# Row maxima of a softmax brought from columns to rows by two DMAs and a ScalarE copy instead of a TensorE transpose

## The chip, the cores and the metric

The kernel runs on one core of one Trainium2 chip. A time is the device time of one execution in microseconds (us); the time of a kernel is the median over its runs. Beside the runs, one execution was taken with the hardware profiler, and all lines of a profile come from it. The engines are TensorE (PE, its weight loads PEld), VectorE (DVE), ScalarE (ACT), GpSimd (POOL) and SyncE (SP). SP does no arithmetic here: it issues nearly all DMAs.

## The reference

One transformer block over 8 batches of 1024 rows of width 256, in float32, with weights given per batch by a small modulation. Cut to what matters:

```python
h = layernorm(x) * (1 + ca) + sa
lhs, rhs = h * w_lhs, h * w_rhs
scores = einsum('nsd,ntd->nst', lhs, rhs)      # 1024 x 1024 per batch, symmetric
attn = softmax(scores, axis=2)
x = x + ga * einsum('nst,ntd->nsd', attn, h)
h = layernorm(x) * (1 + cb) + sb
x = x + gb * (relu(h @ W1 + b1) @ W2 + b2)     # 256 -> 1024 -> 256
```

The softmax takes the maximum of each row of `scores` off before the exponential.

## The kernel before

**Tiles.** A batch has eight row tiles of 128 rows, called rows 0 to 7 of the batch below. The main loop runs over batches `b` (0 to 7) and, in each, over steps `i` (0 to 7). A step works on several stages at once: it computes the scores of the row two ahead (`direct`), mirrors them into the columns of later rows (the score matrix is symmetric), takes the exponentials of the row one ahead, multiplies exponentials by values for earlier rows, and does part of the feed-forward network of the batch before, in eight column chunks `c`, two in each of the steps 0, 1, 4 and 5.

**Layout of the softmax.** `row_max` (line 463, VectorE) takes the maximum of each of the 128 score rows of a tile: one number on each partition, a column. The exponentials, however, are kept turned, with the softmax's row along the free axis, so the maximum is wanted as a row of 128 numbers, the same on all partitions. `max_turn` (line 468) makes it: TensorE transposes the column, read 128 times over, into a PSUM tile `pm`. `subtract` (line 475, VectorE) takes `pm` off the scores into `pT`, and `exponent` (line 484, ScalarE) takes the exponential.

**Where `max_turn` stands.** In step 5 it is called inside `pair_products(fb, fg, c, turn_max)`, the first layer of the feed-forward network. That function issues the products of chunk `c`, has ScalarE copy the first of them to SBUF (`kept`, line 747), and at its end calls what it was given. The order of step 5 from there on, shortened:

```python
pair_products(fb, fg, c, turn_max)      # c = 2; kept, then max_turn of row 6
pair_relu(c - 1)                        # ScalarE, lines 789 and 790
pair_sums(fb, fg, c); mirror(*ahead); pair_last(fb, fg, c)
subtract(*late)                         # row 6
pair_products(fb, fg, c + 1, None)      # c + 1 = 3; kept again
exponent(*late)                         # row 6
...
pair_last(fb, fg, c + 1)                # TensorE writes pa again: needs kept of c + 1
```

`pair_last` multiplies once more into the first half of `pa`, the PSUM tile that `kept` is copied from. So TensorE may issue it only when that copy is done. Behind it stand the products of row 5 (`po`, line 501).

**Where row 6's maximum is taken.** The end of step 4 reads, shortened: `prepare_blocks(b + 1, 1)`, `weights(late)` (row 5), `row_max(b, 6)`. `prepare_blocks` turns the next batch's normalised rows by `move` (lines 306 and 309): four DMAs write the tile `T_a` to DRAM (`D_a`), and one reads it back as `X_a`. All five go on SP's queue, and the read waits there until the four writes have landed. `mirror` and the turns of the feed-forward tensors (`D_f`, `D_y`) go through the same `move`. Batch 7 has no next batch and leaves this `prepare_blocks` out.

**Order.** Nothing is scheduled freely: `pin` at the end ties each instruction to the one before it on its engine, SP's DMAs included, in the order in which the program issued them.

Of the kernel before, what the change touches and what calls it, by code (L numbers as in the profile page):

```python
# [11 lines left out]
F32 = mybir.dt.float32  # L12
# [5 lines left out]
P = 128  # L18
# [6 lines left out]
def adaln_block_kernel(  # L25
# [13 lines left out]
    nc = tc.nc  # L39
    B, S, D = x.shape  # L40
    INTER = W1.shape[1]
    NT = S // P
# [3 lines left out]
    TH = HALF // P  # L46
# [1 line left out]
    NH = NI // 2  # L48
    V = 32
    NV = P // V  # L50
    DX = D + 4

    const = ctx.enter_context(tc.tile_pool(name="const", bufs=1))
    two = ctx.enter_context(tc.tile_pool(name="two", bufs=2))
    work = ctx.enter_context(tc.tile_pool(name="work", bufs=3))
# [3 lines left out]
    dram = ctx.enter_context(tc.tile_pool(name="dram", bufs=1, space=bass.MemoryType.DRAM))  # L59
# [42 lines left out]
    def load_x0(q, queue):  # L102
# [11 lines left out]
        out=wv[ND : 2 * ND, :], in_=w_rhs.rearrange("a b (k p) -> (a b k) p", p=P)  # L114
# [19 lines left out]
    ident = const.tile([P, P], F32, name="ident")  # L134
# [5 lines left out]
    def warm(n):  # L140
# [9 lines left out]
            name=nc.get_next_instruction_name(),  # L150
# [105 lines left out]
    def prepare_start(b):  # L256
        xg_t[b] = two.tile([P, NT, DX], F32, tag="xg", name=f"xg_{b}")
        nc.gpsimd.memset(xg_t[b][:, :, D : D + 1], 1.0)
# [89 lines left out]
    def prepare_turn(b, g, vector=True):  # L348

        xg, pts = xg_t[b], []  # L350
        lT = lT_t[b, g] = two.tile([P, ND, HALF], F32, tag="lT", name=f"lT_{b}_{g}", bufs=2)
        rT = rT_t[b, g] = two.tile([P, ND, HALF], F32, tag="rT", name=f"rT_{b}_{g}", bufs=2)
        rows = lambda T, k: T[:, k, :].rearrange("p (t a v) -> p t a v", a=NV, v=V)
        for k in range(ND):
            if b > 0:
                pt = pre[b, g][:, k]
            else:
                pt = ps_t.tile([P, HALF], F32, tag="t", name=f"pth_{b}_{g}_{k}")
                for j in range(TH):
                    nc.tensor.transpose(pt[:, ts(j, P)], xg[:, g * TH + j, ts(k, P)], ident)  # L360
                pt = pt.rearrange("p (t a v) -> p t a v", a=NV, v=V)
            pts.append(pt)

        def left(k):
            nc.vector.tensor_scalar(
                rows(lT, k), pts[k], side_col(0, 0, k, b), side_col(0, 1, k, b),
                ALU.mult, ALU.add,
            )


        for k in range(ND):
            if vector:
                left(k)
            q = ND - 1 - k if vector else k
            nc.scalar.activation(
                rows(rT, q), pts[q], AF.Identity,
                scale=side_col(1, 0, q, b), bias=side_col(1, 1, q, b),
            )
        return left
# [13 lines left out]
    def score_row(b, i):  # L393
        if b == 0:
            return first_scores()[:, i].rearrange("p (n v) -> p n v", v=V)
        return sc_t[b].rearrange("p i a j v -> p j (i a) v")[:, i]
# [62 lines left out]
    max_t, pT_t = {}, {}  # L459

    def row_max(b, i):
        m = work.tile([P, 1], F32, tag="m", name=f"m_{b}_{i}")
        nc.vector.tensor_reduce(m, score_row(b, i), AX.XY, ALU.max)  # L463
        max_t[b, i] = m

    def max_turn(b, i):
        pm = ps_t.tile([P, HALF], F32, tag="t", name=f"pm_{b}_{i}")
        nc.tensor.transpose(pm[:, :P], max_t.pop((b, i)).to_broadcast([P, P]), ident)  # L468
        pT_t[b, i] = pm

    def subtract(b, i):

        pm = pT_t.pop((b, i))
        pT = work.tile([P, NT, P], F32, tag="pT", name=f"pT_{b}_{i}")
        nc.vector.tensor_tensor(  # L475
            pT.rearrange("p j (a v) -> p j a v", v=V),
            score_columns(b, i),
            pm[:, :P].rearrange("p (j a v) -> p j a v", j=1, v=V).to_broadcast([P, NT, NV, V]),
            ALU.subtract,
        )  # L480
        pT_t[b, i] = pT

    def exponent(b, i):
        nc.scalar.activation(pT_t[b, i], pT_t[b, i], AF.Exp)  # L484
# [24 lines left out]
    def product_out(b, i):  # L509
        po = po_t.pop((b, i))  # L510
        g, j = divmod(i, TH)
        rl = work.tile([P, 1], F32, tag="rl", name=f"rl_{b}_{i}")
        nc.vector.reciprocal(rl, po[:, D : D + 1])
        x2 = x_tile(b, i)
        nc.vector.scalar_tensor_tensor(x2, po[:, :D], rl, x2, ALU.mult, ALU.add)
        stats(mvb_of(b, g), j, x2, f"b{b}_{i}")
# [3 lines left out]


    XS = D - P + 1
    tsum = const.tile([P, 4, TH, P + 4], F32, name="tsum")
    nc.gpsimd.memset(tsum[:, 1, :, P : P + 1], 1.0)

    def right_sums(b, which):

        xg = xg_t[b]
        b11, b12 = xg[:, 0:TH, P:D], xg[:, 0:TH, 0:P]
        b21, b22 = xg[:, TH:NT, P:D], xg[:, TH:NT, 0:P]  # L530
        t = [tsum[:, n, :, 0:P] for n in range(4)]
        ins = [(b12, b11), (b22, t[0]), (b22, b12), (t[1], b21)]
        for n in which:
            nc.gpsimd.tensor_tensor(t[n], *ins[n], ALU.subtract)
# [4 lines left out]
    def pair_begin(b, i, between=None):  # L539

        W = work.tile([P, 2, D + 4], F32, tag="W", name=f"W_{b}_{i}", bufs=1)
        pp = ps_a.tile([P, HALF], F32, tag="a", name=f"pp_{b}_{i}")
        one, other = halves(pT_t[b, i])
        rows = slice(P, P + XS)
        for out, lhs, h in (
            (pp[:, 0:XS], one, 0), (pp[:, XS : 2 * XS], other, 1)
        ):
            for t in range(TH):
                nc.tensor.matmul(  # L549
                    out, lhsT=lhs[:, t, :], rhs=xg_t[b][:, h * TH + t, P : P + XS],  # L550
                    start=(t == 0), stop=(t == TH - 1),
                )
            if between and h == 0:
                between()
        nc.scalar.copy(W[:, 1, rows], pp[:, 0:XS])
        two_t[b, i] = W, pp
# [22 lines left out]
    def pair_end(b, i):  # L579

        (s2, s4), (s3, a22) = halves(pT_t.pop((b, i))), halves(pT_t.pop((b, i + 1)))
        s1 = two_t.pop("s1")
        pq = ps_a.tile([P, HALF], F32, tag="a", name=f"pq_{b}_{i}")
        pr = ps_a.tile([P, HALF], F32, tag="a", name=f"pr_{b}_{i}")
        for out, lhs, rhs in (
            (pr[:, P : 2 * P], s1, tsum[:, 0, :, 0:P]),
            (pq[:, XS : XS + P], a22, tsum[:, 3, :, 0:P]),
            (pr[:, 2 * P : 3 * P], s3, tsum[:, 2, :, 0:P]),
            (pq[:, 0:XS], s2, tsum[:, 1, :, 0:XS]),
            (pr[:, 0:P], s4, xg_t[b][:, TH:NT, 0:P]),  # L590
        ):
            for t in range(TH):
                nc.tensor.matmul(  # L593
                    out, lhsT=lhs[:, t, :], rhs=rhs[:, t, :],
                    start=(t == 0), stop=(t == TH - 1),
                )
        two_t[b, i] = two_t[b, i][0], pq, pr
# [39 lines left out]
    def spare():  # L637
        if queue:
            queue.popleft()()
# [369 lines left out]
    def first_rows():  # L1009

        pr = ps_a.tile([P, HALF], F32, tag="a", name="prow")
        nc.tensor.matmul(
            pr[:, :HALF],
            lhsT=ident[:, 0:1].to_broadcast([P, P]),
            rhs=early_c[:, 0:2, :].rearrange("b j d -> b (j d)"),
            start=True,
            stop=True,
        )
        return pr
# [17 lines left out]
    pr = first_rows()  # L1037
# [106 lines left out]
    def weights(b, i):  # L1144
        subtract(b, i)
        exponent(b, i)

    last_exponent = (0, 1)
    late = None
    for b in range(B):  # L1150
        for i in range(NT):
# [8 lines left out]
            if (b, i) == (0, NT - 2):  # L1160

                prepare_turn(1, 1)
                product(b, i)
                direct(*ahead)
                exponent(*last_exponent)
                product_out(b, i)
                mirror(*ahead)
                early(b, i)
                for _ in range(4):
                    spare()  # L1170
                norms(b, i)
                row_max(*ahead)
                late, last_exponent = ahead, None
                continue
            if ahead and ahead != (0, 2):
                direct(*ahead)
            if b == 0:
# [37 lines left out]
            if first:  # L1215
# [28 lines left out]
                if (b, i) == (1, 0):  # L1244
                    exponent(*late)
                    late = None
# [41 lines left out]
            else:  # L1288
# [5 lines left out]
                if i == 2:  # L1294
                    left_sums(b, 1)
                elif i == 3:
                    pair_begin(b, i, turn_max)
                elif i == 6:
                    pair_begin(b, i, lambda: (max_turn(*late), weights(*late)))
                elif not ahead:  # L1300

                    pair_end(b, i - 1)
                    pair_out(b, i - 1)
                    pair_stats(b, i - 1)
# [64 lines left out]
            late = ahead if ahead != extra else None  # L1369
# [7 lines left out]
    b = B - 1  # L1377
# [74 lines left out]
```

## Time and profile before

| | |
|---|---|
| median of 3 runs | 757.05 us (756.62 to 757.45) |
| the profiled execution | 756.93 us |
| its span from the first to the last instruction | 755.1 us |
| TensorE busy | 749.1 us, 99% of the span |
| VectorE, GpSimd, ScalarE busy | 574.9, 570.9, 374.9 us |
| the max transposes (line 468) | 64, of 274 ns each |
| DMA, mean over 16 engines | 126 GB/s |

Busy times of TensorE overlap: each matmul is listed with its whole latency while the next has begun. What a matmul occupies is read from start to start. In the groups of instructions, a line gives the source line, the engine, the operation, the tile written and the tiles read, the count, and after the bar the busy time in us and the mean of one in ns. In the order of time, a line gives the start in us, the time until its last instruction ends, the engine, the line, the operation and how many instructions were merged.

### The profile page before, as it was taken

The page shows a single profiled execution, that of the slowest core. Times are in us where ns is not written, and L with a number is a line of the kernel's source. Part 1 is how long each engine was busy: PE and PEld are TensorE (multiplying, and loading weights), DVE is VectorE, ACT ScalarE, POOL GpSimd, SP SyncE. Part 2 cuts the span into 40 slices and gives each one's busy share as a digit, 9 for nine tenths or more (in the row PEclk, how much of TensorE's full clock was granted, in tenths as well). Part 3 has the DMA queues.
Part 4 walks back from the last instruction along what each step waited for, and adds up shares of the span by engine and source line. Part 5 has one row for each costly group of instructions (what it writes and reads, how often), then busy time and mean ns, then how long its engine had stood idle before and what let it go on. Part 6 is the DMA issues. An engine that isn't in the chain of part 4 may idle for free.

```text
span 755.1 us, 11883 instructions
## 1 busy us (share of the span) xinstructions
PE 749.1 (99%) x3876; PEld 623.4 (83%) x3876; DVE 574.9 (76%) x1259; ACT 374.9 (50%) x688; POOL 570.9 (76%) x658
## 2 busy tenths in 40 slices
PE   8999999999999999999999999999999999999998
PEld 4686889788897888888888878988889788888887
DVE  7787879778796879968878688876889777685632
ACT  4554646635375454745546444563546535252521
POOL 3762796878968798788877699777996888669741
PEclk9999999999999999999999999999999999999999
DMA  9033442455443453445534555245553354133220
GB/s 308 16 112 98 131 133 74 135 178 152 127 120 123 153 153 110 147 118 158 164 99 119 153 154 161 74 127 172 155 152 85 119 166 133 50 91 126 84 85 28
DMA packets 106213, 95.21 MB, mean 126 GB/s; under 512 B 29700, under 2 KB 98848, under 8 KB 106152
## 3 DMA queue, kind: packets, MB, share of 16 engines
q1 hardware_dynamic: 98408, 85.81, 38.6%
q10 hardware_dynamic: 7744, 8.65, 3.7%
q8 instruction: 30, 0.49, 0.3%
q14 instruction: 31, 0.25, 0.1%
HBM read 50.62 MB, written 43.81 MB: 125 GB/s over the span
## 4 chain that ended last, share of the span: by engine, by line
PE 96%; DMA 1%; DVE 1%; ACT 1%; issue 0%
PE psc L412 16%; PE pa L726 11%; PE po L501 10%; PE pr L593 7%; PE pb L726 7%; PE pc L726 7%; PE yc L806 6%; PE ya L806 6%; PE yb L806 6%; PE pq L593 5%; PE pp L549 5%; PE py L916 4%; PE yd L806 3%; DMA wm<-in_L_wmod_dram 1%; PE pm L468 1%; PE pmr L194 0%
## 5 line engine op out<-in xcount | busy, mean ns | idle before, releaser
L412 PE MATMUL psc<-rT,lT 128*128 128x512 f32 (+3 forms) x384 | 134.8, 487 | 0.0
L780 POOL TENSOR_TENSOR f<-f,kept 128x512 f32<-128x512 f32 x64 | 81.5, 1274 | 42.8 <-DVE f L779 20.1
L419 ACT COPY sc<-psc 128x512 f32<-128x512 f32 (+3 forms) x96 | 44.7, 476 | 119.9 <-PE psc L412 113.0
L484 ACT ACTIVATE pT<-pT 128x1024 f32<-128x1024 f32 x64 | 67.6, 1056 | 70.6 <-DVE pT L475 70.5
L475 DVE TENSOR_TENSOR pT<-sc,pm 128x1024 f32<-128x1024 f32 x64 | 77.3, 1208 | 29.3 <-PE pm L468 13.7
L412 PEld LDWEIGHTS psc<-rT,lT 128*128 128x128 f32 x384 | 66.4, 191 | 37.2 <-issue 25.6
L501 PE MATMUL po<-xg,pT 128*128 128x257 f32 x352 | 80.6, 380 | 0.0
L463 DVE TENSOR_REDUCE m<-sc 128x1 f32<-128x1024 f32 x64 | 77.4, 1209 | 2.2 <-ACT sc L419 1.8
L501 PEld LDWEIGHTS po<-xg,pT 128*128 128x128 f32 x352 | 66.2, 190 | 10.0 <-issue 0.7
L747 ACT COPY kept<-pa 128x512 f32<-128x512 f32 x64 | 37.4, 584 | 69.3 <-PE pa L726 69.1
L726 PE MATMUL pb<-hs,w1s 128*128 128x256 f32 x256 | 65.9, 380 | 0.1
L726 PE MATMUL pc<-hT,w 128*128 128x256 f32 x256 | 65.7, 379 | 0.0
L880 POOL TENSOR_TENSOR x<-x,Y 128x512 f32<-128x512 f32 x28 | 35.1, 1276 | 29.3 <-DMA Y<-D_y 29.3
L789 ACT ACTIVATE f<-f 128x512 f32<-128x512 f32 x64 | 39.8, 622 | 34.7 <-POOL f L780 34.7
L642 POOL TENSOR_TENSOR x<-x,rows 128x256 f32<-128x256 f32 x64 | 44.8, 732 | 13.8 <-ACT rows L1022 10.6
L726 PEld LDWEIGHTS pb<-hs,w1s 128*128 128x128 f32 x256 | 48.5, 190 | 7.3 <-DVE f L765 0.8
L726 PEld LDWEIGHTS pc<-hT,w 128*128 128x128 f32 x256 | 48.6, 190 | 6.7
L806 PE MATMUL yc<-f,w2s 128*128 128x256 f32 x224 | 51.3, 379 | 0.0
L435 DVE STREAM_TRANSPOSE Tm<-sc 128x896 f32<-128x896 f32 (+6 forms) x49 | 34.3, 701 | 20.3 <-ACT sc L419 19.6
L806 PEld LDWEIGHTS yc<-f,w2s 128*128 128x128 f32 x224 | 41.5, 190 | 8.1 <-issue 2.9
L549 PEld LDWEIGHTS pp<-xg,pT 128*128 128x128 f32 x336 | 41.9, 192 | 5.1 <-DVE st_b L241 1.4
L799 POOL TENSOR_TENSOR ft<-f 128x256 f32<-128x256 f32 x56 | 40.8, 729 | 6.8 <-ACT f L790 6.8
(166 smaller groups left out, 1821.1 us busy)
## 6 DMA issues: line engine op xcount, KB each, us to landing
D_f<-T_f SPq DMA_DIRECT2D x60, 128.0 KB, 2.5
X_f<-D_f SPq DMA_DIRECT2D x15, 512.0 KB, 3.7
D_a<-T_a SPq DMA_DIRECT2D x56, 128.0 KB, 2.8
D_y<-T_y SPq DMA_DIRECT2D x56, 128.0 KB, 2.9
Y<-D_y SPq DMA_DIRECT2D x14, 512.0 KB, 3.4
out_dram<-x SPq DMA_DIRECT2D x14, 512.0 KB, 4.4
X_a<-D_a SPq DMA_DIRECT2D x13, 512.0 KB, 3.4
x<-in_L_attn_x_dram ACTq DMA_DIRECT2D x12, 512.0 KB, 3.4
```

The costliest lines, as they stand in the source:

```text
L412: nc.tensor.matmul(psc[:, : hi - lo], lhsT=lT_t[b, i // TH][:, k, ts(i % TH, P)], rhs=rT_t[b, n][:, k, lo - n * HALF : HALF], start=(k == ...
L419: nc.scalar.copy(score_row(b, i)[:, lo // V : hi // V, :], psc[:, : hi - lo].rearrange("p (n v) -> p n v", v=V),)
L463: nc.vector.tensor_reduce(m, score_row(b, i), AX.XY, ALU.max)
L475: nc.vector.tensor_tensor(pT.rearrange("p j (a v) -> p j a v", v=V), score_columns(b, i), pm[:, :P].rearrange("p (j a v) -> p j a v", j=1, ...
L484: nc.scalar.activation(pT_t[b, i], pT_t[b, i], AF.Exp)
L501: nc.tensor.matmul(po[:, : D + 1], lhsT=pT[:, t, :], rhs=xg_t[b][:, t, 0 : D + 1], start=(t == 0), stop=(t == NT - 1),)
L549: nc.tensor.matmul(out, lhsT=lhs[:, t, :], rhs=xg_t[b][:, h * TH + t, P : P + XS], start=(t == 0), stop=(t == TH - 1),)
L593: nc.tensor.matmul(out, lhsT=lhs[:, t, :], rhs=rhs[:, t, :], start=(t == 0), stop=(t == TH - 1),)
L642: queue.append(lambda: nc.gpsimd.tensor_tensor(out, in0, row, op))
L726: nc.tensor.matmul(out, lhsT=lhsT, rhs=rhs, start=True, stop=True)
L780: nc.gpsimd.tensor_tensor(f[:, c::NH, hi], f[:, c::NH, hi], kept[:, None, hi].to_broadcast([P, 2, H2]), ALU.add,)
L806: nc.tensor.matmul(out, lhsT=lhs(c), rhs=rhs(c), start=(c == 0), stop=(c == NH - 1))
```

## The change

From batch 1 on, the maxima don't pass through TensorE. `row_max` adds two DMAs on SP's queue behind the reduction: one writes the 128 numbers to a DRAM tile, the other, which waits for the first, reads the 512 bytes back onto each of the 128 partitions, into `mt`, a tile of 128 x 128 with a single buffer. `max_turn` becomes a ScalarE copy of `mt` into the PSUM tile `pm`; it stands where the transpose stood, save in step 6, where it is brought ahead of `direct`. Batch 0 keeps the transpose. To make room for `mt`, the value tile `xg` has a row of 258 elements in place of 260, and `tsum` pads only the quarter whose padding is used.

```diff
-    DX = D + 4
+    DX = D + 2
...
         max_t[b, i] = m
+        if b == 0:
+            return
+
+        D_ = dram.tile([P], F32, tag="Dm", name=f"Dm_{b}_{i}", bufs=3)
+        nc.sync.dma_start(out=D_, in_=m.rearrange("p o -> (p o)"))
+        max_t[b, i] = work.tile([P, P], F32, tag="mt", name=f"mt_{b}_{i}", bufs=1)
+        nc.sync.dma_start(out=max_t[b, i], in_=D_.partition_broadcast(P))
 
     def max_turn(b, i):
+
         pm = ps_t.tile([P, HALF], F32, tag="t", name=f"pm_{b}_{i}")
-        nc.tensor.transpose(pm[:, :P], max_t.pop((b, i)).to_broadcast([P, P]), ident)
+        m = max_t.pop((b, i))
+        if b == 0:
+            nc.tensor.transpose(pm[:, :P], m.to_broadcast([P, P]), ident)
+        else:
+            nc.scalar.copy(pm[:, :P], m)
         pT_t[b, i] = pm
...
-    tsum = const.tile([P, 4, TH, P + 4], F32, name="tsum")
-    nc.gpsimd.memset(tsum[:, 1, :, P : P + 1], 1.0)
+    tsum = const.tile([P, 4 * TH * P + TH * 4], F32, name="tsum")
+    tsum_first = tsum[:, : TH * (P + 4)].rearrange("p (t d) -> p t d", t=TH)
+    tsum_rest = tsum[:, TH * (P + 4) :].rearrange("p (n t d) -> p n t d", n=3, t=TH)
+    tsum_of = lambda n: tsum_first if n == 1 else tsum_rest[:, n - (n > 1)]
+    nc.gpsimd.memset(tsum_first[:, :, P : P + 1], 1.0)
...
+            if b > 0 and i == NT - 2:
+
+                max_turn(*late)
             if ahead and ahead != (0, 2):
                 direct(*ahead)
...
-                    pair_begin(b, i, lambda: (max_turn(*late), weights(*late)))
+                    pair_begin(b, i, lambda: weights(*late))
```

The hunks left out replace the four uses of `tsum[:, n, ...]` by `tsum_of(n)`.

More of the change, by code (lines that the diff above doesn't have):

```diff
@@ L530, in right_sums @@
         b21, b22 = xg[:, TH:NT, P:D], xg[:, TH:NT, 0:P]
-        t = [tsum[:, n, :, 0:P] for n in range(4)]
+        t = [tsum_of(n)[:, :, 0:P] for n in range(4)]
         ins = [(b12, b11), (b22, t[0]), (b22, b12), (t[1], b21)]
@@ L585, in pair_end @@
         for out, lhs, rhs in (
[L586 to L589, printed above, removed]
+            (pr[:, P : 2 * P], s1, tsum_of(0)),
+            (pq[:, XS : XS + P], a22, tsum_of(3)),
+            (pr[:, 2 * P : 3 * P], s3, tsum_of(2)),
+            (pq[:, 0:XS], s2, tsum_of(1)[:, :, 0:XS]),
             (pr[:, 0:P], s4, xg_t[b][:, TH:NT, 0:P]),
```

## The prediction

> **What bounds the kernel.** First the page: the busy times and the chain that ended last. Then the groups of instructions with shapes kept apart, for the transposes.
>
> ```profile
> PE 749.1 (99%) x3876; PEld 623.4 (83%) x3876; DVE 574.9 (76%) x1259; ACT 374.9 (50%) x688; POOL 570.9 (76%) x658
> ...
> PE 96%; DMA 1%; DVE 1%; ACT 1%; issue 0%
> ```
>
> ```profile
> L468 PE MATMUL pm<-ident,m 128*128 128x128 f32 x64 | 17.5, 274 | 0.0
> ```
>
> TensorE is never without work, so what it no longer does is gained, and whatever makes it wait is lost in full: there is no idle time to take a wait. The transposes look like 17.5 us, but matmuls overlap. What one occupies is read in TensorE's order of time; this is batch 4, step 5:
>
> ```profile
> 402.10 0.27 PE L468 MATMUL pm<-ident,m 128*128 128x128 f32 x1
> 402.21 0.60 PE L726 MATMUL pa<-hT,w1s 128*128 128x256 f32 x2
> ...
> 404.37 1.03 PE L726 MATMUL pc<-hT,w 128*128 128x256 f32 x4
> 405.23 0.59 PE L726 MATMUL pa<-hT,w1s 128*128 128x256 f32 x2
> ```
>
> The transpose of row 6 starts at 402.10 and the next product at 402.21: 0.11 us. At 405.23 stands the `pair_last` of chunk 3, which has to wait for that chunk's `kept`. Now the same moment on VectorE, SP's queue and ScalarE, in this order:
>
> ```profile
> 398.43 1.20 DVE L463 TENSOR_REDUCE m<-sc 128x1 f32<-128x1024 f32 x1
> ...
> 404.14 1.21 DVE L475 TENSOR_TENSOR pT<-sc,pm 128x1024 f32<-128x1024 f32 x1
> ```
>
> ```profile
> 398.96 0.50 SPq L309 DMA_DIRECT2D Y<-D_y  x1
> 399.51 1.91 SPq L306 DMA_DIRECT2D D_a<-T_a  x4
> 404.76 0.34 SPq L309 DMA_DIRECT2D X_a<-D_a  x1
> ```
>
> ```profile
> 400.92 0.58 ACT L747 COPY kept<-pa 128x512 f32<-128x512 f32 x1
> 401.39 0.64 ACT L789 ACTIVATE f<-f 128x512 f32<-128x512 f32 x1
> 401.93 0.62 ACT L790 ACTIVATE f<-f 128x512 f32<-128x512 f32 x1
> 403.76 0.59 ACT L747 COPY kept<-pa 128x512 f32<-128x512 f32 x1 [1.21 <-PE pa L726]
> ```
>
> Row 6's maximum is ready at 399.63 and transposed 2.5 us later. SP stands still from 401.42 to 404.76: the `X_a` read waits for the `D_a` writes. On ScalarE the `kept` copy that frees `pa` ends at 404.35, 0.88 us before TensorE wants it.
>
> [...] nothing leaves SP in those 3.3 us. [...] The start of this trace shows the slow part:
>
> ```profile
> 1.45 2.07 PE L143 MATMUL pw<-early_a 128*128 128x512 f32 x2 [1.45 <-DVE early_a L131]
> ...
> 3.76 2.93 PE L143 MATMUL pw<-early_a 128*128 128x512 f32 x4
> 6.62 2.03 PE L194 MATMUL pmr<-wm,scT 128*8 128x512 f32 x4
> ```
>
> Two products of 512 columns take 2.0 us there, against 0.43 each later (four `psc` in 1.72 us); full speed comes at 6.6. From 1.45 to 6.6, work worth some 2.4 us took 5.2, so 2.8 were lost. No run here yet shows the clock falling within the kernel.
>
> **What is removed.** 56 transposes (batches 1 to 7) of 0.11 us: -6.2 us, full gain if nothing else moves. Their 56 weight loads ran beside matmuls and count nothing.
>
> **What is added, and the place where it decides: rows 6 of batches 1 to 6.** In program order the two new DMAs of row 6 stand behind the whole `prepare_blocks`, thus behind the `X_a` read and its wait. Their prices are bounded by the nearest DMA rows:
>
> ```profile
> X_a<-D_a SPq DMA_DIRECT2D x13, 512.0 KB, 3.4
> ...
> D_m<-Tm SPq DMA_DIRECT2D x28, 16.0 KB, 1.9
> sc<-D_m SPq DMA_DIRECT2D x7, 64.0 KB, 2.3
> ```
>
> The write of 512 bytes: 1.9 us, the smallest landing on the page, if it is alone; up to 3.4 if it lands no sooner than the 512 KB `X_a` read just ahead of it in the queue. I take 2.6. The read is 64 KB, so the row of that size, 2.3; bounds 1.9 and 3.4. Then, in batch 4:
>
> - `X_a` read issued: 404.76 + 0.34 = 405.10
> - write landed: + 2.6 = 407.70; read landed: + 2.3 = 410.00
> - ScalarE copy to `pm`: a copy of the same shape (`sc`, 128x128) takes 247 ns: 410.25
> - behind it the two relus, 401.39 to 402.55, so 1.16: 411.41
> - then `kept` of chunk 3, 0.58: 411.99; TensorE came for it at 405.23.
>
> TensorE stands for 6.76 us. In general it is (`X_a` issue minus `pair_last` issue) + 7.23. That difference, from the orders of time of the six batches, is +0.52, -0.36, -0.93, -0.47, +0.84 and +1.20 us for batches 1 to 6, +0.80 together. Sum: 6 x 7.23 + 0.80 = **+44.2 us**. With 1.9 and 1.9 it is 37.6, with 3.4 and 3.4 it is 55.6. What waits with it: VectorE's `subtract` of row 6 and the sums of chunk 3 behind it, and row 7's maximum; all of these come later by about what TensorE does, so I count nothing for them.
>
> **Ahead of it, step 4.** Row 5's write goes behind the `sc` read at 385.57 (0.53): 386.1 + 2.6 + 2.3 + 0.25 = 391.3. The copy holds the gating of `Y` (389.99) by 1.3 us; the turn `T_y`, begun at 392.08, comes 0.7 later, and all SP work behind it, `X_a` included. I take 0.5 per batch, **+3.0** (0 to 6).
>
> **Clock.** [...] Loss per stall 0 (no drop) to 2.8 (as at the start); I take 2.3: 6 x 2.3 = **+13.8**.
>
> **Other rows.** Row 7 (step 6): its maximum, now after the stall, has SP to itself; 1.9 + 2.3 + 0.25 is close to the 5.4 us between maximum and `subtract` before, and the score evictions behind its copy have 5 us until TensorE needs their PSUM tiles: nothing. Row 0 (step 6 to 7): its read sets the `D_f` writes and all later SP work back, down to the `Y` read of step 7 (348.03), by some 3.8 us; GpSimd's addition of `Y` at 352.51 then starts about 2.9 us late, the relu behind it too, and `kept` of chunk 2 in step 1 has 1.06 us to spare (359.71 against 360.77): 0 to 1 us per batch, **+3.0** for six (0 to 6). Rows 1, 2 and 4 have 7 to 12 us between maximum and `subtract`, and row 3's lateness of about 2 us ends in ScalarE and VectorE gaps of step 3 (4.22 us before 380.70): nothing; without that cover, 2 us per batch. Batch 7 has no `X_a`: the write goes at 670.80, `kept` ends at 670.80 + 4.9 + 0.25 + 1.16 + 0.58 = 677.69 against 676.95: **+0.7**. Batch 1's first two maxima, which share `mt`: **+1** (0 to 3).
>
> **Nothing:** the 56 copies on ScalarE (14 us, half of it idle, save where they wait), SP's issue time (some 0.64 us a row, SP idle more than half), 3.6 MB more on DMA engines that are about 45% busy, and the two layout edits: same shapes, other strides. No row shows a price by stride; a loss would show as longer `po` or `tsum` rows on TensorE or GpSimd, a gain likewise, and I give it 0, within 2 us either way.
>
> **Sum:** -6.2 + 44.2 + 3.0 + 13.8 + 3.0 + 0.7 + 1 = +59.5. On the profiled execution (756.93, of which 755.1 is the span) that is 816.4; the median is 0.1 higher. **Forecast 816 us.** The low ends give -6.2 + 37.6 = +31.4, 788 us; the high ends -6.2 + 55.6 + 6 + 16.8 + 6 + 0.7 + 3 = +81.9, 839 us.
>
> **Rivals.**
> - *The stall without the clock drop:* 816 - 13.8 = 802 us. For it: no drop is on record within this kernel. [...] Chance 0.31; the forecast has 0.54.
> - *Round trip only:* the new DMAs are not held by `X_a`. Row 6 then goes from 399.63 to 399.63 + 4.9 + 0.25 + 1.16 + 0.58 = 406.5, a stand of 1.3 us, six times 7.7 - 6.2: 758, no measurable change. Against it stands the program order of SP. Chance 0.03.
> - *Faster, on the other side:* the column is on all partitions before ScalarE needs it, and 56 x 0.11 us is all that happens: 750.7 us. It decides at `kept` done by 405.2, so `mt` landed by 405.2 - 0.58 - 1.16 - 0.25 = 403.2, which is 3.6 us after the maximum. Even two smallest landings (3.8) miss that without `X_a` in front. What speaks for it: TensorE's 99%, and VectorE's 13.7 us of waiting for `pm`. Chance 0.04.
> - *More stalls:* rows 0, 1 and 3 also stop TensorE, since each mirror queue is now longer by two waits: above 839, say 850. Chance 0.08.
>
> The range 786 to 838 holds the forecast and the first rival nearly whole. About 0.2% (1.5 us) is what can be told from no change here: slower 0.54 + 0.31 + 0.08 = 0.93, same 0.03, faster 0.04.
>
> **What would show it.** After: TensorE idle before `pa` (line 726) in step 5, some 7 us, six times, put down to ScalarE's `kept`; ScalarE idle ahead of the copy into `pm`, put down to the DMA into `mt`; on SP the write of `m` right behind each second `X_a` read; matmuls of double length after each stall, if the clock falls. I am wrong if the write of `m` leaves before `X_a`, if TensorE's idle time at `pa` stays under 10 us in all, or if `kept` of chunk 3 is not what it waits for.

## The result, and the profile after

The changed kernel takes 1230.65 us (median of 4 runs, 1229.08 to 1240.07) against 757.25 us for the kernel before on the same chip. The ratio is 1.627, with a 95% interval of 1.624 to 1.630. The forecast was 816 us, with a range of 786 to 838: the sign was right, the size was wrong by a factor of eight (+473 us in place of +59.5).

The page of the changed kernel: busy times, the chain that ended last (its shares by engine), and two of the costliest groups, with the idle time just before them after the last bar.

```profile
PE 885.2 (72%) x3820; PEld 707.7 (58%) x3820; DVE 574.3 (47%) x1259; ACT 383.4 (31%) x744; POOL 567.4 (46%) x658
...
DMA 32%; DVE 8%; issue 5%; PE 5%; POOL 4%; ACT 3%; SPq 2%; DVEq 0%; ACTq 0%; POOLq 0%
...
L741 PE MATMUL pa<-hT,w1s 128*128 128x256 f32 x128 | 58.3, 551 | 221.5 <-ACT kept L762 221.5
L480 ACT COPY pm<-mt 128x128 f32<-128x128 f32 x56 | 15.1, 269 | 590.3 <-DMA mt<-Dm 590.3
```

The kernel is no longer bound by TensorE. Before, TensorE held 96% of the chain; now it holds 5%, and DMAs are the largest part of it. (The shares add up to 59%, since the profile follows this chain back only to 493 us after the start.) The span grew from 755.1 to 1230.3 us, by 475.2. TensorE's idle time (span minus busy) accounts for 339.1 of that (6.0 before, 345.1 after). The other 136.1 is TensorE's busy time, which rose from 749.1 to 885.2 although 56 transposes are gone. Its granted clock is 0.834 over the span, 1.000 before.

The idle time has the form that the forecast named: TensorE stands before `pa` for ScalarE's `kept` (221.5 us), and ScalarE stands before the copy into `pm` for the DMA into `mt` (590.3 us). But there are 28 of these stalls in front of `pa`, not 7: those of row 6 in batches 1 to 6 make 77.6 us of the 221.5, those of row 5 make 61.0, and most of the rest are rows 1 and 2.

SP's queue in the table of waits, and the two new DMAs in the table of DMA issues (last number: median us from issue to landing):

```profile
SPq L471 <- DMA Dm<-m: 409.7, 56, 9.3
```

```profile
mt<-Dm SPq DMA_DIRECT2D x56, 64.0 KB, 4.1
...
Dm<-m SPq DMA_DIRECT2D x56, 0.5 KB, 7.6
```

The smallest DMA of the kernel, 512 bytes, lands more than twice as late as the 512 KB read of `X_a` did before (3.4 us). SP, which the forecast called idle for more than half of the time, stands 409.7 us for it. All of SP's waits for DMAs together went from 185.1 to 643.2 us, +458.1 where the span grew by 475.2.

Row 6 of batch 4, in the order of time of SP's queue, of ScalarE and of TensorE; this is the place that the prediction worked out:

```profile
653.31 0.34 SPq L309 DMA_DIRECT2D X_a<-D_a  x1
653.69 0.43 SPq L469 DMA_DIRECT2D Dm<-m  x1
662.77 0.32 SPq L471 DMA_DIRECT2D mt<-Dm  x1
663.20 0.39 SPq L898 DMA_DIRECT2D out_dram<-x  x1
671.94 0.32 SPq L469 DMA_DIRECT2D Dm<-m  x1
```

```profile
666.88 0.27 ACT L480 COPY pm<-mt 128x128 f32<-128x128 f32 x1 [15.69 <-DMA mt<-Dm]
...
668.13 0.56 ACT L762 COPY kept<-pa 128x512 f32<-128x512 f32 x1
```

```profile
668.75 1.22 PE L741 MATMUL pa<-hT,w1s 128*128 128x256 f32 x2 [13.43 <-ACT kept L762]
669.76 6.01 PE L513 MATMUL po<-xg,pT 128*128 128x257 f32 x16
```

The write leaves right behind the `X_a` read, as forecast. It takes 9.08 us until the read behind it is issued and 4.11 more until ScalarE can copy, where the forecast had 2.6 and 2.3. From the issue of `X_a` to the end of `kept` it is 15.38 us, not 7.23. After the stall the matmuls are slow: the 16 `po` products take 6.01 us; they took 3.63 before. The clock granted from 668.7 to 672.0 us is 0.50.

### The profile page after: what moved, and what is told of

It reads as the page before. It is cut to its first block, busy times and chain, and to the rows that moved or that the text cites. A ratio compares the mean times of both kernels' runs of the same rounds, so it can differ in the third digit from the quotient of the medians.

```text
span 1230.3 us, 12055 instructions
## 1 busy us (share of the span) xinstructions
PE 885.2 (72%) x3820; PEld 707.7 (58%) x3820; DVE 574.3 (47%) x1259; ACT 383.4 (31%) x744; POOL 567.4 (46%) x658
## 4 chain that ended last, share of the span: by engine, by line
DMA 32%; DVE 8%; issue 5%; PE 5%; POOL 4%; ACT 3%; SPq 2%; DVEq 0%; ACTq 0%; POOLq 0%
DMA Dm<-m 18%; DMA mt<-Dm 10%; DMA D_m<-Tm 2%; DVE m L463 2%; DVE pT L487 2%; POOL tsum L549 1%; SPq L306 1%; PE py L931 1%; DMA D_a<-T_a 1%; POOL f L795 1%; DVE T_y L882 1%; PE pa L741 1%; SPq L309 1%; PE ya L821 1%; PE pp L564 1%
## 5 line engine op out<-in xcount | busy, mean ns | idle before, releaser
L741 PE MATMUL pa<-hT,w1s 128*128 128x256 f32 x128 | 58.3, 551 | 221.5 <-ACT kept L762 221.5
L480 ACT COPY pm<-mt 128x128 f32<-128x128 f32 x56 | 15.1, 269 | 590.3 <-DMA mt<-Dm 590.3
L741 PEld LDWEIGHTS pa<-hT,w1s 128*128 128x128 f32 x128 | 29.6, 257 | 235.7 <-ACT kept L762 232.7
L513 PE MATMUL po<-xg,pT 128*128 128x257 f32 x352 | 106.6, 467 | 12.2 <-ACT pT L496 12.2
L513 PEld LDWEIGHTS po<-xg,pT 128*128 128x128 f32 x352 | 86.0, 247 | 32.4 <-ACT pT L496 12.9
L729 POOL TENSOR_TENSOR hs<-hT 128x256 f32<-128x256 f32 x16 | 11.7, 729 | 176.8 <-DVE hT L720 176.8
L580 POOL TENSOR_TENSOR s<-pT 128x512 f32<-128x512 f32 x21 | 26.7, 1269 | 133.6 <-ACT pT L496 133.6
L741 PE MATMUL pb<-hs,w1s 128*128 128x256 f32 x256 | 74.7, 418 | 8.2 <-DVE W L576 6.6
L564 PE MATMUL pp<-xg,pT 128*128 128x129 f32 x336 | 62.4, 363 | 24.8 <-DVE Y L843 24.8
L564 PEld LDWEIGHTS pp<-xg,pT 128*128 128x128 f32 x336 | 60.7, 274 | 32.8 <-ACT pT L496 28.9
L741 PEld LDWEIGHTS pc<-hT,w 128*128 128x128 f32 x256 | 52.4, 208 | 26.0 <-DVE Y L865 18.1
```

What stands on the lines that cost most here:

```text
L513: nc.tensor.matmul(po[:, : D + 1], lhsT=pT[:, t, :], rhs=xg_t[b][:, t, 0 : D + 1], start=(t == 0), stop=(t == NT - 1),)
L564: nc.tensor.matmul(out, lhsT=lhs[:, t, :], rhs=xg_t[b][:, h * TH + t, P : P + XS], start=(t == 0), stop=(t == TH - 1),)
L580: nc.gpsimd.tensor_tensor(s1, *halves(pT_t[b, i + 1]), ALU.add)
L741: nc.tensor.matmul(out, lhsT=lhsT, rhs=rhs, start=True, stop=True)
```

## The experiments

Numbers of lines differ from kernel to kernel; the tiles' names don't. "Before" is always the kernel before, measured beside the run (757.1 to 757.7 us). "E1" and so on are names for this text only.

**E1: the layout edits alone.** `tsum` and `xg` as changed, row 7's turn at its earlier place, but TensorE transposes all rows.

```diff
-        D_ = dram.tile([P], F32, tag="Dm", ...)      # and both DMAs
...
-            nc.scalar.copy(pm[:, :P], m)
+        nc.tensor.transpose(pm[:, :P], m.to_broadcast([P, P]), ident)
```

> Only the two layout edits (value rows of 258 elements, the packed sums tile) and the earlier place of the max in step 6; the maxima still go through TensorE and no DMA is added. The forecast gave these edits 0 within 2 us: 755 to 759 us. If the strides of the value tile carry part of the 473 us, this run is clearly above 760.

Measured: 757.92 us, ratio 1.0006 (0.9997 to 1.0014). The edits around the change cost nothing.

**E2: the transposes gone, and nothing waited for.** ScalarE copies a constant tile instead of `mt`; there are no new DMAs. VectorE multiplies by it where it subtracted. The maxima are left out of the computation.

```diff
-        nc.sync.dma_start(out=D_, ...); nc.sync.dma_start(out=max_t[b, i], ...)
+        max_t[b, i] = level        # a constant on all partitions
...
-            ALU.subtract,
+            ALU.subtract if b == 0 else ALU.mult,
```

> No transposes and no DMAs from batch 1 on: ScalarE copies a constant tile into PSUM, and VectorE multiplies by it where it subtracted the maximum (the maxima are left out). This is the change with its DMAs free. The forecast's first term: 56 x 0.11 = 6.2 us gained, 751 us. If the ScalarE copies themselves (56 x 0.25 us) hold TensorE, it is 757 or above.

Measured: 757.6 us, ratio 1.0006 (0.9994 to 1.0018). So even with DMAs that cost nothing at all, this change would have given nothing measurable. Yet the gain is there for a while. The products of row 5 (`po`) in step 5 of batches 4 to 7 begin at 405.67, 496.10, 586.55 and 677.38 us before, and at 402.68, 493.23, 583.66 and 674.51 here. That is 3.0 us ahead in batch 4 (0.3 of it already in batch 0), by 0.6 to 0.8 per batch, where eight transposes of 0.11 us would be 0.9. From there on the period is the same as before, and the span ends nearly level (754.5 against 755.1). The table of TensorE's waits of this kernel begins:

```profile
PE ya L818 <- ACT Y L830: 2.7, 4, 1.0
```

TensorE now waits for ScalarE's copy of `Y`, once in each of batches 4 to 7. In batch 4's order of time these lead up to that copy, one behind the other, from the landing of `X_a` on: ScalarE's work on `X_a`, four relus, the copy into `pm`, row 7's `subtract` on VectorE (which waits 1.8 us for `pm`), the score evictions, the exponential. Before, TensorE waited at that place once, in batch 7, for 0.3 us, so its next limit was close. But the copy that replaces the transpose stands in this chain itself. So the second branch of the expectation, that the copies on ScalarE hold TensorE, is not excluded: no run leaves out both the transposes and the copies. TensorE's busy time fell by 3.8 us, and its idle time rose by 3.2. Why the busy time fell by 3.8 and not by 6.2 is not explained.

**E3: both DMAs, and nobody uses them.** The DMAs run on SP as in the change; TensorE transposes all rows.

```diff
-        max_t[b, i] = work.tile([P, P], F32, tag="mt", ...)
-        nc.sync.dma_start(out=max_t[b, i], in_=D_.partition_broadcast(P))
+        mt = work.tile([P, P], F32, tag="mt", ...)
+        nc.sync.dma_start(out=mt, in_=D_.partition_broadcast(P))
...
-            nc.scalar.copy(pm[:, :P], m)
+        nc.tensor.transpose(pm[:, :P], m.to_broadcast([P, P]), ident)
```

> The two DMAs of each row run as in the change, but nothing reads what they bring; TensorE makes the maxima as before. Theory A, the wait of the copy on ScalarE costs the time: 757 to 800 us, with the write still landing after 7 to 9 us. Theory B, the SP queue costs it: SP's own waits and issues before the change come to about 48 us of the 91 us of a batch, 8 x 8.1 more make 113, so each of 7 batches is 22 us longer: about 910 us.

Measured: 1157.92 us in one run. Some 400 us, where the change costs 473, are there with no ScalarE copy and with no computing engine that waits for `mt`. So most of the loss needs only the two DMAs and SP's queue, not the copies. The size of it was beyond both expectations: the write's landing is 8.8 us here.

**E4: the write in four pieces.** VectorE turns the column in blocks of 32 (0.21 us), so that the write is four pieces of 128 bytes instead of 128 pieces of four. It goes to the same 512 bytes of DRAM, and the read is the same.

```diff
-        nc.sync.dma_start(out=D_, in_=m.rearrange("p o -> (p o)"))
+        nc.vector.transpose(turned, m.to_broadcast([P, V]))
+        nc.sync.dma_start(out=D_, in_=turned[0:P:V, :])
```

> As the change, but VectorE first turns the column in blocks of 32, so that the write to DRAM is 4 pieces of 128 bytes instead of 128 pieces of 4; the read is as it was. Theory C, the 128 pieces of 4 bytes make the write slow: it lands in about 2 us instead of 7 to 9, the read in 2.3 to 4.1, and the kernel takes 800 to 860 us, near the forecast of 816, with the longest stalls at row 6. Theory D, the write lands late for what stands ahead of it in the queue, or because it goes to one place of 512 bytes: it still takes 6.5 us or more and the kernel is above 1100 us.

Measured: 897.83 us, ratio 1.185 (1.181 to 1.190). SP waits 115.0 us for the 56 writes, 2.1 each, in place of 409.7. The form of the write, with all that hangs on it, is worth 333 us of the 473; the remaining 140 are there with a fast write too. That is theory C's fast write, but the time is above its 800 to 860 us. The longest stalls before `pa`, 5.1 to 8.0 us, are those of row 6, as expected.

**E5: four-byte pieces, 512 bytes apart.** To tell the size of the pieces from their place: 128 pieces of four bytes again, but each in a row of its own, read back as such. The result is not used.

```diff
-        D_ = dram.tile([P], F32, tag="Dm", ...)
-        nc.sync.dma_start(out=D_, in_=m.rearrange("p o -> (p o)"))
+        D_ = dram.tile([P, P], F32, tag="Dm", ...)
+        nc.sync.dma_start(out=D_[:, 0:1], in_=m)
...
+        nc.sync.dma_start(out=mt[:, 0:1], in_=D_[:, 0:1])
```

> As the run with unused results, but each 4-byte piece goes to a place of its own, 512 bytes from the next, and the read brings the same 4-byte pieces back to 128 partitions. Theory C1, the size of the pieces makes the write slow: it still lands after 7 us or more, and the time stays near 1158 us. Theory C2, it is slow because all pieces go into the same 512 bytes: it lands in 2 to 3.5 us, and the time is 800 to 900 us.

Measured: 789.83 us in one run, a little below theory C2. Its DMA issues:

```profile
Dm<-m SPq DMA_DIRECT2D x56, 0.5 KB, 2.8
...
mt<-Dm SPq DMA_DIRECT2D x56, 0.5 KB, 1.6
```

As many pieces, as small, land in 2.8 us when they lie apart. So neither their number nor their size makes the landing late by itself. Neither does the 512-byte place by itself, since four pieces into it are fast (E4: SP waits 2.1 us for them). In these runs it took both: many small pieces into one place. What else may differ between the writes, such as how many DMA engines share one, was not varied alone. (The read differs from E3's as well, so the whole time isn't a pure comparison with E3; the landing of the write is.)

**E6: the slow write alone.** As E3 without the read, so that no DMA depends on the write (the profile still puts 23.4 us of SP's waits down to it). The result is not used.

```diff
-        max_t[b, i] = work.tile([P, P], F32, tag="mt", ...)
-        nc.sync.dma_start(out=max_t[b, i], in_=D_.partition_broadcast(P))
```

> As the run with unused results, but the write alone, without the read that waits for it. Theory B, SP's wait for the landing holds up all DMAs behind it: with no wait nothing is held, 757 to 765 us. Rival, the slow write itself blocks the DMA engines: several tens of us above that, up to the 1158 us of the run with the read.

Measured: 925.25 us in one run, +168. Theory B alone, 757 to 765 us, falls; this is within what the rival named. A DMA issue of this kernel, then a wait of SP:

```profile
D_f<-T_f SPq DMA_DIRECT2D x60, 128.0 KB, 9.4
```

```profile
SPq L309 <- DMA D_f<-T_f: 110.9, 26, 10.9
```

Before, `D_f` landed in 2.5 us and SP waited 32.8 us for it. So the slow write delays other DMAs, which have nothing to do with it: `D_f`, issued behind it, lands as late as the write itself, 9.4 us against 9.5. What holds `D_f` up is not shown by a run, and neither is why pieces in one place are slow.

**E7: row 6 only, fast write.** E4's DMAs for row 6 alone; TensorE transposes the rest.

```diff
-        if b == 0:
+        if b == 0 or i != 6:        # in row_max and in max_turn
```

> The write in 4 pieces and the broadcast read for row 6 of batches 1 to 7 alone; all other maxima by TensorE. The forecast's main term at the prices found since (write 3.2, read 2.9): 6 x (7.23 + 1.2) + 0.8 = 51.4 us of standing, and 6 x 2.3 for the clock, less 0.8 for seven transposes: about 821 us. If TensorE does not stand at row 6 as forecast, or the clock does not fall, it is below 800.

Measured: 820.2 us, ratio 1.083 (1.081 to 1.086), against 821 from the forecast's term at the landings found before (3.2 and 2.9 us). All seven stalls of TensorE are where the forecast put them. The first of them:

```profile
142.03 1.22 PE L745 MATMUL pa<-hT,w1s 128*128 128x256 f32 x2 [8.29 <-ACT kept L766]
```

Batches 1 to 6 stand for 8.29, 7.02, 7.75, 7.30, 8.34 and 7.70 us, 46.4 together. The forecast had 44.2 with 2.6 us for the write and 2.3 for the read. In this run it is 2.7 from the issue of the write to that of the read (median of seven) and 2.9 for the read; with these the same sum gives 48.5. Batch 7 stands for 1.30 (forecast 0.7). TensorE's busy time rises by 14.9 us with seven transposes less (0.8), so 15.7 us of slower matmuls, 2.6 for each of the six long stalls (forecast 2.3). That the total of 821 is met so closely is in part luck: it had 51.4 us of standing, 5.0 too many, and 1.9 too few for the slow matmuls. The clock is seen directly in batch 4: granted 1.00 from 425 to 436 us, before the stall, 0.50 from 443.2 to 446.0, behind it, and 1.00 again from 449.

**E8: all rows but 6, fast write.** The complement of E7.

```diff
-        if b == 0:
+        if b == 0 or i == 6:
```

> The same for all rows but row 6. The forecast counted almost nothing for these rows: 757 to 763 us. Rival: each row's wait sets SP's queue back, the lateness is handed on from row to row, and the copies on ScalarE stand for it: the rest of the 141 us of the run with four pieces, 800 to 850 us.

Measured: 835.05 us, ratio 1.104 (1.098 to 1.109). The forecast had some 7 us for these rows, "nothing" for most of them; they cost 78 us. E7 and E8 together give 63 + 78 = 141 us, E4 gave 140, so the two parts add up. The longest stalls are those of row 5. Batch 4's, in the order of time of VectorE, of SP's queue, of ScalarE and of TensorE:

```profile
426.68 0.21 DVE L469 STREAM_TRANSPOSE turned<-m 128x32 f32<-128x32 f32 x1
```

```profile
420.70 0.34 SPq L473 DMA_DIRECT2D mt<-Dm  x1
421.08 1.88 SPq L307 DMA_DIRECT2D D_a<-T_a  x4
425.46 0.34 SPq L310 DMA_DIRECT2D X_a<-D_a  x1
425.90 1.81 SPq L307 DMA_DIRECT2D D_m<-Tm  x4
429.98 0.57 SPq L310 DMA_DIRECT2D sc<-D_m  x1
430.60 0.54 SPq L471 DMA_DIRECT2D Dm<-turned  x1
```

```profile
435.48 0.27 ACT L484 COPY pm<-mt 128x128 f32<-128x128 f32 x1 [7.10 <-DMA mt<-Dm]
```

```profile
438.15 1.22 PE L745 MATMUL pa<-hT,w1s 128*128 128x256 f32 x2 [4.75 <-ACT kept L766]
```

The `mt` read of row 4 leaves at 420.70, and only behind it go the four `D_a` writes, the `X_a` read, and the mirror's writes and read. Row 5's maximum is ready at 426.64, but its write leaves at 430.60, 3.96 us later. In the kernel before, the mirror's read left 0.13 us after that maximum (385.57 against 385.44), so the forecast gave row 5 a free queue, 0.66 us after. Then the copy on ScalarE holds the gating of `Y` and `kept` behind it. The lateness of one row did not run out in the gaps of VectorE and ScalarE; SP handed it on to the next row.

**E9: rows 2, 4 and 5, fast write.** Two rows to which the forecast gave the most room, and row 5.

```diff
-        if b == 0:
+        if b == 0 or i not in (2, 4, 5):
```

> The four-piece DMAs and the ScalarE copy for rows 2, 4 and 5 only. By the forecast these rows have 7 to 12 us between maximum and subtract (row 5 less) and cost nothing, and three transposes of 0.11 us less in each of seven batches could give up to -2.3 us: 755.2 to 757.5. If row 5's copy is late whatever the other rows do (as the 4.5 to 5.2 us per batch before pa in the run of all rows but 6 suggest), 785 to 800. If row 5 was late there only because rows 3 and 4 had set SP back, below 765.

Measured: 777.24 us, ratio 1.026 (1.024 to 1.028), between the expectations. Row 5 is late again with only rows 2 and 4 before it: TensorE stands 14.1 us for `kept`, 13.6 of it in step 4, up to 4.4 at once. In E8 it stood 26.8 us there. So half of row 5's lateness is gone without the other rows. Row 5 alone was not run.

**E10: row 6 only, with the change's own write.** E7's condition, with the DMAs of the change.

```diff
-        if b == 0:
+        if b == 0 or i != 6:
```

> The change as it was made, with its own two DMAs (128 pieces of four bytes into one place, then the spread), but for row 6 alone; the other rows are transposed by TensorE. If only the landings were mis-sized in the forecast's term for row 6, that term with the measured landings gives the time: (X_a minus pair_last) + 7.23 + (7.6 - 2.6) + (4.1 - 2.3) = 14.03 us per batch, 84.2 + 0.8 for batches 1 to 6, 0.7 + 6.8 = 7.5 in batch 7, clock 13.8 to 16.8, -0.8 for seven transposes: 757.5 + 105.5 to 108.5 = 863 to 866, say 855 to 875, with stalls of about 14 us before pa in step 5. If the slow write costs more than its own landing, because it sets back DMAs of other queues that row 6 doesn't wait for, the time is above 880. If the spread's 4.1 us came from the traffic of the other rows, it is about 2 us less per batch, some 850.

Measured: 868.47 us, ratio 1.146 (1.145 to 1.148); the landings are 8.4 and 4.3 us. TensorE stands seven times; the first is

```profile
149.09 1.22 PE L741 MATMUL pa<-hT,w1s 128*128 128x256 f32 x2 [15.28 <-ACT kept L762]
```

and batches 1 to 6 sum to 86.4 us, where the forecast's sum says 85.0 with the landings of the changed kernel and 87.5 with what this run shows (7.8 from the issue of the write to that of the read, 4.3 for the read). Batch 7 stands 8.30 (7.5). So at row 6 the mechanism was right and the landings were mis-sized. Slower matmuls add 18.9 us (18.1 more busy time, 0.8 of transposes gone), 2.7 per stall, for stalls of 8 to 15 us.

E7 and E10 have the same row and the same queue and differ in the write, so they show where its time goes. The profile lists a DMA's packets. In batch 4 of E10 the write is issued at 454.78 us, right behind the `X_a` read, and SP issues the read that waits for it at 463.13. The packets of all DMA engines of the core from 454.7 to 457.4 us, then from 457.4 to 463.1:

```profile
DMA packets 288, 0.52 MB, mean 194 GB/s; under 512 B 160, under 2 KB 160, under 8 KB 288
```

```profile
DMA packets 0, 0.00 MB, mean 0 GB/s; under 512 B 0, under 2 KB 0, under 8 KB 0
```

Of the 288 packets, 128 are the `X_a` read; the 160 small ones have four bytes each, the 128 pieces among them. No packet moves in the last 5.7 us, and SP still waits for the write. In both kernels the last packet ends 2.56 us after the issue of the write (median of seven). From there SP stands 5.32 us more in E10 and 0.16 in E7. The 128 pieces take no longer to move than the four; what is late is their completion, the moment from which SP can go on.

**E11: E8's DMAs, unused.** TensorE transposes all rows, ScalarE copies nothing.

```diff
-        max_t[b, i] = work.tile([P, P], F32, tag="mt", ...)
+        mt = work.tile([P, P], F32, tag="mt", ...)
...
-        if b == 0 or i == 6:
+        if True:                    # in max_turn: all rows by TensorE
```

> The four-piece DMAs for all rows but row 6, as in the run that gave 835.05, but nobody uses what they bring: TensorE transposes all rows and ScalarE copies nothing. If the 78 us of that run come from SP's queue (waits that set the other DMAs back), it stays at 820 to 840. If they come from ScalarE, whose copies wait for mt and hold the evictions behind them, it is at 757 to 765. In between, the shares are read off: what remains above 757.5 is SP's.

Measured: 782.94 us, ratio 1.033 (1.028 to 1.039). Of E8's 78 us, 26 are there without any engine using `mt`; they come from the DMAs, SP's queue and VectorE's turns of the column together. The other 52 are only there when ScalarE's copies wait for `mt`. With a fast write, then, the copies are the larger part; with the slow one (E3) most of the loss is there without them.

**E12: rows 2 and 4 only, fast write.** What remains if row 5 is left to TensorE too.

```diff
-        if b == 0:
+        if b == 0 or i not in (2, 4):
```

> The four-piece DMAs and the ScalarE copy for rows 2 and 4 only. With row 5 as well the time was 777.24. If row 5 alone was to blame there (its copy holds kept ahead of pa), this run is level with the kernel before, 756 to 759, and up to 14 x 0.11 = 1.5 us faster at best. If rows 2 and 4 cost something too, because their waits on SP's queue set the mirror and block DMAs behind them back or their copies hold ScalarE's evictions, it is at 762 to 772.

Measured: 756.18 us (12 runs, 755.02 to 756.55) against 757.4, ratio 0.9982 (0.9974 to 0.9991). This is 1.2 us faster than the kernel before; fourteen transposes at 0.11 us are 1.5. All that TensorE waits for in the steady part is one line:

```profile
PE pa L745 <- ACT kept L766: 0.4, 1, 0.4
```

## Why the prediction was wrong

**Right.** The sign. The place and mechanism at row 6: the write behind `X_a`, ScalarE's copy waiting for `mt`, `kept` behind it, TensorE before `pa`. None of the three signs that would have refuted it appeared. E7 and E10 confirm its sum at two different landing times: with the landings of the run itself it gives 48.5 where 46.4 us were measured, and 87.5 where 86.4 were. That E7's 46.4 is so close to the forecast's 44.2 is in part luck, since the landings were longer. The clock's part was right in size, 2.6 and 2.7 us per long stall where 2.3 was taken, and the granted clock is seen to fall to 0.50, so the rival without a clock drop falls. That a stall of this length would lower it was the author's estimate before the runs; that the slow start has the same cause is not shown. (The start of the trace would have given 2.6 as well: six products at 0.43 us are 2.6 us of work, not 2.4, so 2.6 of the 5.2 were lost there.) In the whole changed kernel the slower matmuls come to 142.3 us (136.1 more busy time, and 6.2 for the transposes), over some 60 stalls of very different length, 2.3 each. The layout edits cost nothing (E1).

**Wrong: "The write of 512 bytes: 1.9 us, the smallest landing on the page ...; up to 3.4".** This step failed first and cost the most. It took the price from DMAs of more bytes, as if fewer bytes could only be faster. The nearest row was not near: 16 KB of `D_m` are 128 pieces too, but of 128 bytes each (four from each of 32 partitions), and they don't share one 512-byte place. The write measured 7.6 us (2.6 taken) and the read behind it 4.1 (2.3 taken). What is late is the completion of the write, not its moving (E10), and no landing on the page before had shown that. At row 6 this makes 111 us (E10) of what is 63 with a fast write (E7). In the whole kernel it makes 333 of the 473 us, the difference between the change and E4. A second effect was in no step at all: the late write delays other DMAs on the queue (E6: `D_f` from 2.5 to 9.4 us, +168 without any dependent read).

**Wrong: "Other rows ... nothing", and "SP's issue time (..., SP idle more than half)".** With fast writes these rows cost 78 us (E8). The forecast followed each row through a queue that stood as in the profile before, and let a lateness end in the next gap of ScalarE or VectorE. But `pin` keeps the queue in order, its own waits for landings are in series, and two more were put into it per row. Before, SP waited 185.1 us for DMAs and 306.4 for VectorE's tiles. The second kind looked like free time, but it does not lie where the maxima come: in E8 row 5's finds SP in the wait for the mirror's writes, and its write leaves 3.96 us later. "More stalls" was on record as a rival at 850 us with a chance of 0.08. Its mechanism (queues longer by two waits per row) is what E8 shows, though beside row 6 it is rows 5, 2 and 1 that stop TensorE before `pa`, not 0, 1 and 3; its size still rested on the same landings.

**Wrong: "-6.2 us, full gain if nothing else moves".** E2 shows that it isn't there even when nothing waits for a DMA: from batch 4 on another chain held TensorE, at a place where it had waited 0.3 us before, and the new copy on ScalarE is part of that chain. A TensorE busy for 99% of the span doesn't say that the next limit is far away. E12 shows a part of the gain, 1.2 us, when fourteen transposes go and their DMAs fit.

**How it adds up.** Of the 473 us, row 6 alone gives 111 (E10). The other 362 are the other rows and what they do to one another with the slow write; with a fast one they cost 78. Within the 362 the shares of SP's wait and of the DMAs held up behind the write are not separated: E3 and E6 give +400 and +168 for the two together and for the second alone, but with other work waiting in each.

## What to carry to other kernels

Price a small DMA by its pieces and where they land, not by its bytes: a column of 128 partitions written to 512 contiguous bytes was the slowest transfer of the changed kernel's main loop (7.6 us), and turning it first into four rows of 32 took nearly three quarters of SP's waiting for it away (409.7 to 115.0 us). Before putting a dependent pair of DMAs into an in-order queue, lay the whole queue out anew, landing after landing, for all iterations, since lateness is handed on there and a gap read from the old profile may have moved. And before counting a saving on the bound engine in full, look for the wait of some tenths of a microsecond that shows which chain comes next.

## What the runs showed of the hardware

- 128 pieces of four bytes from 128 partitions into one 512-byte place in DRAM landed in 7.6 to 9.5 us (medians of four kernels: the changed one, E3, E6 and E10); 512 bytes apart in 2.8 (E5). For four pieces of 128 bytes into such a place SP waited 2.1 us on average (E4).
- The lateness was in the completion, not in the moving: the last packet ended 2.56 us after the issue in E10 (128 pieces) and in E7 (four), and SP could go on 5.32 and 0.16 us after it.
- In E6 the late write also delayed the landing of DMAs issued behind it: `D_f` from 2.5 to 9.4 us, `D_y` from 2.9 to 8.5, `D_a` from 2.8 to 6.6.
- A stall of TensorE cost 2.6 us on top of itself, as slower matmuls after it, where the stalls were 7 to 8 us long (E7), and 2.7 where they were 8 to 15 (E10). The granted clock behind one was 0.50 (E7, batch 4, and the changed kernel, batch 4).
